# Sums over states taken first by the scheduler, four products in a row, in a decoder layer with a state-space scan

## The chip, the core and the metric

The kernel runs on one core of a Trainium2 chip. A core has five engines that work side by side, each on its own queue: PE (TensorE, matmuls, with its weight loads shown apart as PEld), DVE (VectorE), ACT (ScalarE), POOL (GpSimd) and SP (SyncE, here the issuer of most transfers). The metric is the device time of one execution in microseconds; the number given for a kernel is the median of its runs.

## The reference

One decoder layer on 8 sequences of 512 positions with 512 channels, all in float32. It has three parts, each with a residual and a layer norm:

```python
x = _layernorm(x + mamba(x))                   # state-space layer
x = _layernorm(x + cross_attention(x, ctx))    # 16 heads of 32
x = _layernorm(x + mixture_of_experts(x))      # 32 experts, 4 for each token, and a shared one
```

The part that the change touches is the state-space layer. With 1024 inner channels d and 16 states n, over the positions t:

```python
xz = layernorm(x) @ in_proj_w;  x_main, z = split(xz)
x_main = silu(conv(x_main))
dt, B_ssm, C_ssm = split(x_main @ x_proj_w);  dt = softplus(dt @ dt_proj_w + dt_proj_b)
dA  = exp(A * dt)                              # for each channel and state
dBx = dt * B_ssm * x_main
h_t = dA_t * h_(t-1) + dBx_t                   # for each channel and state
y_t = sum over n of h_t[d, n] * C_t[n]
y = (y + x_main * D) * silu(z)
out = y @ out_proj_w
```

## The kernel before

**How the work is tiled.** The scan goes through 16 chunks: 8 sequences, each in two chunks of T = 256 positions. A chunk has 32 steps (q, g, jj). q (4 values) picks 256 of the 1024 channels, g (4 values) picks one state out of each of four groups, and jj (2 values) picks half of the channels of q. One tile h of a step has 128 partitions, 32 channels times 4 state groups, and 4 blocks of 256 positions beside one another, each with one column in front for the carried state.

**A step** is a chain on three engines. `decays` (ACT, line 482, four instructions) makes exp(A dt) in one of two buffers `das`. `carry` (ACT, line 490) takes a new h buffer, one of six, and puts the carried state in its first columns. `steps_in` (DVE, line 496) writes dt B x into h. `scan` (DVE, line 503) runs the recurrence over the whole tile. `keep` (ACT, line 508) saves the last column. `collect` (DVE, line 512) multiplies h by C in place.

**The sums over states.** `collect` is called with jj = 0 and then with jj = 1. The first call only remembers h; the second hands back a function, `products`, that is called one step later. It sums over the states with PE: `fold` is a 128 x 32 matrix of ones and zeros that adds the four state groups of each channel. A group has four products of line 523 ("quarters"). Quarters 0 and 1 read the h of jj = 0, quarters 2 and 3 that of jj = 1, and quarter j writes the 32 partitions from 32 j on of the PSUM tile `py`. Over the four g the products add up in `py`, and before the first of them one product with the identity (line 521) starts it from x D. There is one `py` buffer; `gated` (DVE, line 537) multiplies z by it when all four g are in, and then the next q may start. Each float32 matmul is recorded as two instructions, so 256 groups of four products are 2048 records. An h buffer is free for `carry` and `steps_in` of a later step when its quarters have read it.

**What runs beside the scan.** In the main loop each step also issues parts of other work, in three thirds (`run(0)`, `run(1)`, `run(2)`): the next chunk's norm, transposes, input projection (line 345) and convolution (379), the products for dt (`prepare`, line 439, for the next q), the output projection of the chunk before (554), and the cross attention, gate and shared expert of the sequence before. Of the attention, `maximum` makes scores on PE (816) and takes their maxima on DVE (818), `subtract` sends the maxima back into a row of the queries by a transfer, `weigh` makes the scores again (833) and their exponentials on ACT (837), and `gather` multiplies by the values (849); the values tile has columns of ones, so that the sums of softmax come out of the same product and reach their place by transfers (869, 871). Dense products of attention and the shared expert are line 752. The parts are paced by hand: each has a weight, and a step issues as many as its share of the two chunks allows.

**What sets the order.** The program is written in one stream, and a scheduler fixes the order of every engine's queue when the kernel is built. It steps through the program in a model of the chip, and among the instructions of an engine that are ready in it takes the one with the best priority; without more said, that is the earliest in the program. On the chip each queue then runs in the fixed order, and an instruction that waits for another engine holds those behind it. Here `products()` stands after `run(1)` of the step that follows its `collect`, so what the parts of `run(2)` and of the next `run(0)` and `run(1)` put on PE is earlier in the program than the products.

Of the kernel before, what the change touches and what calls it, by code (L numbers as in the profile page):

```python
# [30 lines left out]
NQ = 4  # L31
# [55 lines left out]
def layers(ctx, tc, a, x1d, filld, based, xbuf):  # L87
# [23 lines left out]
    nc = tc.nc  # L111
# [374 lines left out]
    def carry(t, q, g, jj):  # L486

        last = state[:, q, g, jj].unsqueeze(2)
        h = mp.tile([P, NB, T + 1], F32, tag="h", name="h", bufs=6)
        nc.scalar.copy(h[:, :, 0:1], last if t else nothing)  # L490
        return h
# [18 lines left out]
    def collect(f, q, g, jj, h):  # L510

        nc.vector.tensor_tensor(h[:, :, 0:T], h[:, :, 1:], f["bc", g][1], ALU.mult)  # L512
        if jj == 0:
            f["half"] = h
            return
        hs, xs = (f.pop("half"), h), f["xs"][q]

        def products():
            if g == 0:
                f["py"] = psy.tile([P, 2, T], F32, tag="py", name="py")  # L520
                nc.tensor.matmul(f["py"], ident, xs, start=True, stop=False)
            for j in range(NQ):
                nc.tensor.matmul(  # L523
                    f["py"][j * QP : (j + 1) * QP, :, :],
                    fold,
                    hs[j // 2][:, 2 * (j % 2) : 2 * (j % 2) + 2, 0:T],
                    start=False,
                    stop=g == NG - 1,
                )

        return products

# [170 lines left out]
    def sources(b):  # L703

        st, todo = {}, []

        def begin():
            load("Wv")
            st["cT"] = cT = quad("s2", "cT")
            nc.sync.dma_start(cT, rows(a["ctx"][b]))  # L710
            st["mk"] = mk = p1.tile([P, S], U8, tag="mk", name="mk")
            nc.sync.dma_start(mk, a["mask"][b : b + 1, :].to_broadcast([P, S]))
            kept[b] = [dp.tile([S, D], F32, tag="vd", name="vd"), dp.tile([D, S], F32, tag="kd", name="kd")]

        def values(pc):
            if pc == 0:
                load("Wk")
            w, cT = loaded["Wv"], st["cT"]
            ps = dense(lambda dc: cT[:, dc, pc * P : (pc + 1) * P], lambda dc: w[:, dc, :])

            def put():
                v = p3.tile([P, D], F32, tag="row", name="v")
                nc.scalar.copy(v, ps)
                nc.sync.dma_start(kept[b][0][pc * P : (pc + 1) * P, :], v)

            return put

        def keys(oc):
            if oc == 0 and b:
                load("Wq")  # L730
            w, cT = loaded["Wk"], st["cT"]
            ps = dense(lambda dc: w[:, dc, oc * P : (oc + 1) * P], lambda dc: cT[:, dc, :])

            def put():

                k = p3.tile([P, D], F32, tag="row", name="k")
                nc.vector.scalar_tensor_tensor(k, ps, bk[:, oc : oc + 1], st["mk"], ALU.add, ALU.mult)
                nc.sync.dma_start(kept[b][1][oc * P : (oc + 1) * P, :], k)

            return put  # L740

        todo.append((0, begin, False))
        for j in range(SC):
            todo.append((3.4, lambda j=j: values(j), False))
        for j in range(DC):
            todo.append((3.4, lambda j=j: keys(j), False))
        return todo
# [298 lines left out]
    def do(fn, *args, first=False):  # L1046

        if first:
            dry(False)
        rest = fn(*args)  # L1050
        settle()
        if rest:
            left.append(rest if isinstance(rest, tuple) else (0, rest))
# [6 lines left out]
    def work(k):  # L1060

        front = 6.9 if k in (2, 3) else 3.4 if 4 <= k < 8 or k in (12, 14, 17, 20, 23) else 1.0 if k in (11, 25) else 0.0
        return 1.2 + front
# [24 lines left out]
    ahead, products = carry(0, 0, 0, 0), None  # L1088
# [3 lines left out]
    for i, (b, t) in enumerate(chunks):  # L1092
        nf = {}
        after = chunks[i + 1] if i + 1 < len(chunks) else None
        if t == 0:
            side, spent = units(b - 1) if b else sources(0), 0.0

            own = [work(k) for k in range(len(steps))] * 2
            whole = sum(own) + sum(x[0] for x in side)
        for k, (q, g, jj) in enumerate(steps):  # L1100
            if i and k == 1:
                bcast(f, NG - 1)
            if after and 28 <= k < 31:
                bcast(nf, k - 28)
            qf, nq = (f, q + 1) if q + 1 < CC // 2 else (nf, 0)
            h = ahead

            parts = []

            def part(fn, *args, first=False):  # L1110
                parts.append((do, fn, *args, first))

            if k in (2, 3) and old:
                part(back, k - 2, *old)
            if 4 <= k < 8:
                part(gate_x, k - 4, f)
            if k == 8:
                parts.append((finish_silu, f["zs"]))
            if k % 8 == 0 and q + 1 < CC // 2:
                part(prepare, q + 1, f)  # L1120
            if k == 25 and after:
                part(prepare, 0, nf)
            if after:
                if k == 8:
                    part(norm_x, nf)
                if k == 11:
                    for j in range(DC // 2):
                        part(flip_x, j, nf)
                if k in (12, 14, 17, 20):
                    part(convolve, after[1], (12, 14, 17, 20).index(k), nf, first=(k == 12))  # L1130
                if k == 22:
                    parts.append((finish_silu, *nf["xs"].values()))
                if k == 23:
                    part(x_proj, nf)
            if side and (k >= 4 or t and k < 2):
                at = t * len(steps) + k + 1
                while side and spent + sum(own[:at]) <= whole * at / len(own):
                    w, fn, alone = side.pop(0)
                    spent += w
                    part(fn, first=alone)  # L1140
            thirds = [[], [], []]
            for m, x in enumerate(parts):
                thirds[round((m + 0.5) * 3 / len(parts) - 0.5) if x[0] is do else 1].append(x)

            def run(m):
                clock[0] += 1
                settle()
                for x in thirds[m]:
                    if x[0] is do:
                        do(*x[1:-1], first=x[-1])  # L1150
                    else:
                        x[0](*x[1:])

            steps_in(f, q, g, jj, h)
            more = qf is f or after
            if k % 8 == 6 and more:
                repeat(qf, nq, 0, 1)
            if k % 8 == 1:
                if k > 1:
                    gated(q - 1, f)  # L1160
                elif old:
                    gated(CC // 2 - 1, old[2])
            if i == 0 and k == 0:
                load("Wo")
            if i == 0 and k == 2:
                biases()
            if k == 0 and old:
                twice_x(*old)
            if k == 5 and after:
                load_x(*after, nf)  # L1170
            run(0)
            scan(das[n % 2], h)
            n += 1

            if k + 1 < len(steps) or after:
                then = steps[(k + 1) % len(steps)]
                ahead = carry(t if k + 1 < len(steps) else after[1], *then)
                decays(f if k + 1 < len(steps) else nf, *then, das[n % 2])
                if k % 8 == 5 and more:
                    repeat(qf, nq, 0, 0)  # L1180
                    repeat(qf, nq, 1, 0)
                if k % 8 == 6 and more:
                    repeat(qf, nq, 1, 1)
            if held:
                keep(*held)
            held = t, q, g, jj, h
            run(1)

            if products:
                products()  # L1190
            products = collect(f, q, g, jj, h)
            run(2)
            while i < 2 and cleared < E * (i * len(steps) + k - 6) // (2 * len(steps) - 7):
                clear(cleared)
                cleared += 1
        while t and side:
            _, fn, alone = side.pop(0)
            do(fn, first=alone)
        old = (b, t, f)
        f = nf  # L1200
# [356 lines left out]
```

## Time and profile before

| | |
|---|---|
| median of 3 runs | 5468.24 us (5460.69 to 5471.74) |
| profiled execution | 5457.57 us, span 5455.9 us |
| mean granted TensorE clock | 0.925 |
| PE busy in the span | 4714.7 us (86%), 17064 instructions |
| DVE busy | 4212.0 us (77%), 5257 instructions |
| ACT busy | 2561.9 us (47%), 5617 instructions |
| stage of the scans | from the start to 3565 us |
| experts and last norm | from about 3850 us to the end |

The span is the time from the first to the last instruction; the execution has 1.7 us around it. The shares are means over stages with different limits: in the scan stage DVE is the busier engine, in the experts' stage PE. Of the six line numbers of a scan step, 482, 490 and 508 are ACT's, 496, 503 and 512 DVE's; 521 and 523 are PE's. A wait in the profile is idle time of an engine, put down to the instruction that ended it.

### The profile page before, as it was taken

To read this page: it belongs to the slowest core of one execution; us is meant where nothing else is said; L and a number is where in the kernel's file an instruction comes from. 1 tells how busy PE (TensorE), PEld (TensorE's weight loads), DVE (VectorE), ACT (ScalarE), POOL (GpSimd) and SP (SyncE) were. 2 spreads that over 40 slices of the span, in tenths; PEclk is the share of its full clock that TensorE was granted. 3 is DMA by queue.
4 is the path that set the end of the run, shared out by engine and by line. 5 is a ranking of instruction groups with operands and counts; after the bars stand their busy time and mean duration, and the time that the engine had idled before them with its cause. 6 is when DMAs were issued, how large, how long until landed. Compare 5 with 4: busy or idle time off the path is not lost. (4 is left out here: it accounts for less than half of the span.)

```text
span 5455.9 us, 53341 instructions
## 1 busy us (share of the span) xinstructions
PE 4714.7 (86%) x17064; PEld 2524.5 (46%) x17064; DVE 4212.0 (77%) x5257; ACT 2561.9 (47%) x5617; POOL 487.8 (9%) x428
## 2 busy tenths in 40 slices
PE   6768888888888888988888888788999999999994
PEld 3324334334433423433343342333677777777773
DVE  7999888888988989898898898943465556665554
ACT  5566465555655556555565655512222222222223
POOL 1000001001000100100100010010111111111111
PEclk8879989899998998998898998898999999999997
DMA  8875336345444634634543463441344444444444
GB/s 239 266 215 145 96 91 203 76 121 162 120 106 111 197 77 108 191 92 107 171 123 98 107 195 77 106 141 48 119 124 125 121 118 120 127 127 120 128 114 143
DMA packets 500889, 719.53 MB, mean 132 GB/s; under 512 B 130577, under 2 KB 215089, under 8 KB 498560
## 3 DMA queue, kind: packets, MB, share of 16 engines
q1 hardware_dynamic: 464592, 627.68, 40.1%
q0 software_dynamic: 33280, 76.90, 7.3%
q10 hardware_dynamic: 2736, 11.54, 0.5%
q8 instruction: 136, 2.23, 0.2%
q14 instruction: 145, 1.19, 0.1%
HBM read 399.63 MB, written 165.31 MB: 104 GB/s over the span
## 5 line engine op out<-in xcount | busy, mean ns | idle before, releaser
L482 ACT ACTIVATE l_da<-rep,l_aneg 128x256 f32<-128x256 f32 x2048 | 897.5, 500 | 886.0 <-DVE h L503 791.7
L503 DVE TENSOR_TENSOR_SCAN h<-l_da,h 128x1028 f32<-128x1028 f32 x512 | 1165.4, 2290 | 6.8 <-ACT l_da L482 3.9
L496 DVE TENSOR_TENSOR h<-rep,bc 128x1024 f32<-128x1024 f32 x512 | 613.0, 1216 | 132.5 <-PE py L523 78.2
L512 DVE TENSOR_TENSOR h<-h,bc 128x1024 f32<-128x1024 f32 x512 | 618.1, 1215 | 1.4
L816 PE MATMUL ps_s<-l_ka,l_qa 64*128 64x512 f32 x1024 | 349.8, 762 | 206.7 <-DVE mx L818 202.0
L523 PE MATMUL py<-h,l_fold 128*32 128x512 f32 x2048 | 400.6, 665 | 95.4 <-DVE h L512 90.7
L1307 PE MATMUL ps_h<-xT,w 128*128 128x320 f32 x1536 | 436.2, 434 | 0.0
L1387 POOL DMA_INDIRECT based<-y,xe x160 | 255.4, 1597 | 1311.5 <-ACT y L1410 578.8
L818 DVE TENSOR_REDUCE mx<-ps_s 128x2 f32<-128x1024 f32 x256 | 309.6, 1215 | 64.1 <-PE ps_s L816 62.1
L1328 DVE TENSOR_TENSOR hT<-ps_h,p 128x320 f32<-128x320 f32 x128 | 63.0, 492 | 378.9 <-PE ps_h L1307 378.9
L1307 PEld LDWEIGHTS ps_h<-xT,w 128*128 128x128 f32 x1536 | 292.7, 191 | 118.5 <-issue 0.8
L816 PEld LDWEIGHTS ps_s<-l_ka,l_qa 64*128 64x128 f32 x1024 | 144.0, 316 | 418.7 <-DVE mx L818 325.2
L837 ACT ACTIVATE eT<-ps_t 128x1024 f32<-128x1024 f32 x256 | 259.7, 1014 | 149.0 <-PE ps_t L833 148.0
L833 PE MATMUL ps_t<-l_qa,l_ka 64*128 64x512 f32 x1024 | 305.8, 675 | 26.5 <-ACT eT L837 13.6
L849 PE MATMUL po<-eT,l_va 128*64 128x512 f32 x1024 | 296.0, 658 | 32.3 <-ACT eT L837 28.7
L1307 PE MATMUL ps_h<-t,s 128*128 128x320 f32 x1024 | 286.1, 432 | 0.0
L345 PE MATMUL ps_z<-xnT,wm 128*128 128x256 f32 x1024 | 241.1, 392 | 22.0 <-DVE o L563 15.8
L554 PE MATMUL po<-wm,zs 128*128 128x512 f32 x512 | 240.2, 620 | 21.8 <-DVE z L950 13.5
L345 PE MATMUL ps_x<-xnT,wm 128*128 128x256 f32 x1024 | 251.9, 399 | 4.3 <-ACT xnT L334 2.5
L345 PEld LDWEIGHTS ps_x<-xnT,wm 128*128 128x128 f32 x1024 | 198.7, 198 | 84.7 <-issue 36.3
L345 PEld LDWEIGHTS ps_z<-xnT,wm 128*128 128x128 f32 x1024 | 195.9, 195 | 87.4 <-DVE o L563 29.2
L752 PE MATMUL ps_p<-x2T,wa 128*128 128x512 f32 x512 | 235.6, 613 | 0.7 <-DVE hT L935 0.7
(227 smaller groups left out, 7116.1 us busy)
## 6 DMA issues: line engine op xcount, KB each, us to landing
w<-in_w SPq DMA_DIRECT2D x93, 1024.0 KB
wm<-in_in_proj_w SPq DMA_DIRECT2D x128, 512.0 KB
rep<-dt SPq DMA_DIRECT2D x256, 256.0 KB
rep<-dtx SPq DMA_DIRECT2D x256, 256.0 KB
xbuf<-zero SPq DMA_DIRECT2D x32, 1362.5 KB
xe<-xbuf SPq DMA_DIRECT2D x32, 1362.5 KB
wm<-in_out_proj_w SPq DMA_DIRECT2D x64, 512.0 KB
wa<-in_sw SPq DMA_DIRECT2D x24, 1024.0 KB
```

The lines of the kernel that those rows point to most:

```text
L345: nc.tensor.matmul(ps[:, i, :], w[:, dc, i * P : (i + 1) * P], f["xnT"][:, dc, :], start=(dc == 0), stop=(dc == DC - 1),)
L482: nc.scalar.activation(da[:, n, 1:], dt[:, j, i, :], AF.Exp, scale=aneg[:, 2 * q + i, 2 * jj + j, g : g + 1])
L496: nc.vector.tensor_tensor(h[:, :, 1:], dtx.rearrange("p j i t -> p (j i) t"), f["bc", g][0], ALU.mult)
L503: nc.vector.tensor_tensor_scan(flat, da.rearrange("p n t -> p (n t)"), flat, 0.0, ALU.mult, ALU.add)
L512: nc.vector.tensor_tensor(h[:, :, 0:T], h[:, :, 1:], f["bc", g][1], ALU.mult)
L523: nc.tensor.matmul(f["py"][j * QP : (j + 1) * QP, :, :], fold, hs[j // 2][:, 2 * (j % 2) : 2 * (j % 2) + 2, 0:T], start=False, stop=g == N ...
L816: nc.tensor.matmul(ps[:, j, :], own, ka[r, :], start=True, stop=True)
L818: return lambda: nc.vector.tensor_reduce(mx[:, :, lt].unsqueeze(2), ps, AX.X, ALU.max) and None
L833: nc.tensor.matmul(ps[:, j, :], ka[r, kc * P : (kc + 1) * P], qa[r, :], start=True, stop=True)
L837: nc.scalar.activation(eT, ps, AF.Exp)
L849: nc.tensor.matmul(po[j * 2 * HD : (j + 1) * 2 * HD, :], va[:, kc, i, j * HD : (j + 2) * HD], eT[:, j, :], start=(kc == 0), stop=(kc == SC ...
L1307: nc.tensor.matmul(ps, w[:, n, r * P : (r + 1) * P], x[:, n, :], start=not more and n == 0, stop=n == 1, skip_group_check=more,)
```

## The change

```diff
             if g == 0:
                 f["py"] = psy.tile([P, 2, T], F32, tag="py", name="py")
                 nc.tensor.matmul(f["py"], ident, xs, start=True, stop=False)
-            for j in range(NQ):
-                nc.tensor.matmul(
+
+            def quarter(j):
+                return nc.tensor.matmul(
                     f["py"][j * QP : (j + 1) * QP, :, :],
                     fold,
                     hs[j // 2][:, 2 * (j % 2) : 2 * (j % 2) + 2, 0:T],
                     start=False,
                     stop=g == NG - 1,
                 )
+
+            with tc.issue_after(quarter(NQ - 1).ins):
+                for j in range(NQ - 1):
+                    quarter(j)
...
             if products:
-                products()
+                with tc.high_priority():
+                    products()
             products = collect(f, q, g, jj, h)
```

The four products of a group are issued in the order 3, 0, 1, 2. `issue_after` puts the three behind the first in PE's queue: an order of issue, not a wait for its end. Quarter 3 reads the h of jj = 1, so no product of a group is issued before both h are there. `high_priority` gives all that `products()` issues, the product with the identity among it, a priority ahead of everything else: the scheduler takes it as soon as it is ready in its model. The products of the very last step, after the loop, are called without it. What is computed, the tiles and their number of buffers stay as they are.

## The prediction

> **What bounds the kernel now.** I read the busy time by stage first. Its columns are the stretch, its length, the busy microseconds of PE (matmuls), PEld (weight loads), DVE, ACT and POOL with counts, then the granted clock and the DMA figures.
>
> ```profile
> 0.00:400.00 400.00, 270.22 (x820) 121.76 (x822) 359.47 (x358) 236.98 (x569) 31.96 (x54) 0.79 0.84 243
> 400.00:3565.00 3165.00, 2674.55 (x9280) 1169.97 (x9277) 2835.43 (x3016) 1815.66 (x4000) 168.60 (x179) 0.92 0.46 125
> 3565.00:3850.00 285.00, 237.26 (x714) 102.00 (x713) 94.14 (x165) 56.40 (x70) 31.83 (x35) 0.89 0.33 110
> ```
>
> The scans run until 3565 us; what follows (the last sequence's attention, the experts, the last norm) holds no product of line 523, so the change acts on the first two rows. From 400 on, where attention runs between the scan steps, DVE is busy 2835.43 of 3165 us (90%) and PE 2674.55 (85%). DVE is the longer queue, and it stands idle for 3165 - 2835.43 = 329.6 us. In the first 400 us there is hardly any attention beside the scans; once they have started, DVE has no gap worth a change.
>
> Second, the costly groups, which give the pace of a scan step:
>
> ```profile
> L503 DVE TENSOR_TENSOR_SCAN h<-l_da,h 128x1028 f32<-128x1028 f32 x512 | 1165.4, 2290 | 6.8 <-ACT l_da L482 3.9
> L496 DVE TENSOR_TENSOR h<-rep,bc 128x1024 f32<-128x1024 f32 x512 | 613.0, 1216 | 132.5 <-PE py L523 78.2
> L523 PE MATMUL py<-h,l_fold 128*32 128x512 f32 x2048 | 400.6, 665 | 95.4 <-DVE h L512 90.7
> ```
>
> The scan itself hardly waits. The multiplication that opens a step (496) waits 132.5 us, and 78.2 of it is for the products: it writes one of six h buffers, which is free only when the products have read it. The 2048 product records are 256 groups of four products, two records to a product.
>
> Third, who waits for whom. The first three lines are DVE's from 45 to 3565 us, the fourth is PE's over the same time, the fifth PE's from 45 to 400 us (total us, times, longest):
>
> ```profile
> DVE h L496 <- PE py L523: 78.2, 48, 4.5
> DVE h L496 <- DMA rep<-dtx: 47.0, 11, 12.1
> DVE mx L818 <- PE ps_s L816: 24.7, 38, 1.3
> ...
> PE ps_s L816 <- DVE mx L818: 195.3, 96, 5.3
> ...
> PE py L523 <- DVE h L512: 80.0, 28, 8.2
> ```
>
> PE waits for DVE's maxima 195.3 us, and DVE waits for PE's products: each stands still while work that the other needs is queued behind. ACT's copy of the carried state (490) waits another 136.1 us for the same products, 100 times, but ACT is busy 58% of the stage and the scan waits only 3.9 us for it.
>
> Fourth, PE's order of time in the middle of a sequence:
>
> ```profile
> 1459.65 1.06 PE L523 MATMUL py<-h,l_fold 128*32 128x512 f32 x8
> 1460.65 1.13 PE L833 MATMUL ps_t<-l_qa,l_ka 64*128 64x512 f32 x4
> ...
> 1467.74 1.25 PE L816 MATMUL ps_s<-l_ka,l_qa 64*128 64x512 f32 x4 [2.67 <-DVE mx L818]
> 1468.92 1.04 PE L523 MATMUL py<-h,l_fold 128*32 128x512 f32 x2
> 1469.89 1.13 PE L833 MATMUL ps_t<-l_qa,l_ka 64*128 64x512 f32 x4
> ...
> 1475.01 1.06 PE L523 MATMUL py<-h,l_fold 128*32 128x512 f32 x6
> 1476.00 1.25 PE L816 MATMUL ps_s<-l_ka,l_qa 64*128 64x512 f32 x4
> ```
>
> Two things are to be seen. Four products in a row (x8) hold PE from 1459.65 to 1460.65, 1.00 us. One alone (x2, at 1468.92) holds it 0.97 us, and its three sisters (x6, at 1475.01) 0.99: they run side by side, and a group that is torn apart costs 0.97 + 0.99 - 1.00 = 0.96 us more. And the group torn here had its second h ready at 1437.56 (end of its multiplication, line 512, in DVE's order of time): it ran 31 to 38 us late, behind attention work, 2.67 us of it spent waiting for a maximum. At 1476.10 DVE starts the 496 that had waited for it. Read off for all 256 groups, the products end 21 us after their second h on the mean, and 30 to 40 us late through the middle of every sequence; 63 groups are torn.
>
> **The change, part by part.** No instruction is added or removed and no DMA moved by hand. The order on the queues changes.
>
> (a) Products first. The wait of 496 (78.2) and that of 537, the gating that reads py (7.2 in all, 6 times), sum to 85.4 us of DVE idleness. With the products next on PE as soon as h is ready, six buffers are ample: a group needs two, and a lag of a few us replaces one of 30. I take the whole 85.4 as removed. Bounds: 0, if DVE only moves on to the next thing that PE brings late, and 85.4.
>
> (b) What is late next. PE's other work now lies behind each group. What DVE needs next of PE is above all the scores for a maximum (816 to 818). Today 38 of the 224 maxima in this stage find PE late, 17%. 223 groups start after 400 us; if 17% of them push a score by their 1.00 us in front of a waiting maximum, that is 223 x 0.17 x 1.00 = 38 us back. Bounds: nothing, if DVE is busy elsewhere each time, and 223 us, if each group does it. I take 38, since the share comes from the same wait.
>
> (c) Four side by side. 63 x 0.96 = 60 us less PE time. I cost it at nothing: the cover is DVE's 2835 us against PE's 2675. If PE set the end it would be worth up to 60.
>
> (d) The wait added. Quarters 0 and 1 read the first h and could start early; now all four wait for the second. PE stands at the group until line 512 is done, and attention's matmuls, the projections and the dt products (439) queue behind; DVE's maxima, ACT's exponentials and the next pair's dt wait for those. The trace has such waits in plenty from 45 to 400 us: 80.0 us in 28, 2.9 each, and DVE lost nothing by them, since nothing behind was due. After 400 us they are 90.7 - 80.0 = 10.7 us in 39 - 28 = 11, 1.0 each. At 1.0 for 223 groups PE is held 223 us, against 3165 - 2675 + 60 = 550 us of idle time: hidden. At 2.9 it is 647, which is 97 more than there is. I take the nearer row, after 400 us, where attention runs: nothing on the path. The range keeps the 97.
>
> A cost of holding PE is its clock. The rows above grant 0.79 in the first 400 us with PE idle a third of the time, 0.92 afterwards with 15% idle. Were the clock of the long stretch to fall to 0.79, its 2675 - 60 us would become 2615 x 0.92 / 0.79 = 3045, still under 3165: no cost by itself, but it uses up most of PE's slack. The Trainium skill ("TensorE: Matmul & The Clock Gate", Part 1) puts it otherwise: the clock drops by half only after an idle window of about 3.4 us. By that rule holds of 1.0 or 2.9 us would leave the clock alone and this item would be zero. The mean clock in these rows cannot tell the two apart.
>
> The sum: -85 + 38 + 0 + 0 = -47 us. The profiled execution has a span of 5455.9 and 5457.6 with what lies around it, so 5411 for such a run. The median of the runs, 5468.2, stands 10.7 above it; I put the forecast against the median: 5468 - 47 = **5421 us**.
>
> **The rivals.**
>
> *The wait only moves.* PE still takes everything else in its old order, and the next pair's dt (439, then ACT, DVE and a transfer) is queued among it. DVE arrives sooner and waits for the transfers of dt and dtx (47.0 us now), for line 455 (38.0) or for scores. For it: PE's backlog of 30 us is attention work, which does not shrink. Against it: much of that backlog is PE waiting 195.3 us for maxima that a freer DVE would give sooner. If all 85 come back: 5468, give or take 15.
>
> *PE is held at its head* (the slower side). By (d), if the mean hold of a group passes (3165 - 2615) / 223 = 2.5 us, PE becomes the bound of the stage. At 2.9 the end moves by 97: 5565; halfway between hold and slack, about 5510. For it: the 28 early waits are that long, and a group now has to follow DVE closely. Against it: those early waits stood where PE had nothing else to do, and the order is chosen so that other work fills the time before h is ready.
>
> *Attention slips past the scans.* Scans that no longer brake for PE can outrun attention's share. What is left at 3565 us runs in a stage where PE is busy 237 of 285 us (83%) and DVE a third: each us of slipped PE work costs 1 / 0.83 = 1.2 there. The stretch from 400 on holds seven of the eight sequences, 2615 / 7 = 374 us of PE for each; a fifth of one slipping, 75 us, costs 90 and gives 5421 + 90 = 5511. It outweighs the gain from 47 / 1.2 = 39 us on.
>
> *It does nothing*: the new order turns out as the old, since buffers rather than preference set it: 5468. The 30 us of lateness speak against that.
>
> **How the numbers follow.** Chances: forecast 0.50, wait only moves 0.16, PE held 0.17, attention slips 0.14, nothing 0.03. A measurement of this kernel can tell about 0.2%, 11 us, from no change. The forecast is faster throughout; of the moved wait I give 0.05 to faster, 0.05 to no difference and 0.06 to slower; the held PE and the slip are slower; doing nothing counts as no difference. So faster 0.55, no difference 0.08, slower 0.37. The forecast's own range is 5468 - 85 - 38 = 5345 (all of (a), none of (b), and 38 of the 60 in (c)) to 5457. For 8 in 10 the range must reach the slower cases too: up to 5540, which takes in the slip and most of the held PE short of its end of 5565.
>
> **What would show it.** Right: the wait of 496 for py falls from 78.2 to under 15 us, and ACT 490's from 136.1 with it; every group stands as x8; the lag of a group behind its second h falls from 21 us to a few; DVE's idle time from 400 us on falls from 330 to about 280; the wait of 818 for scores rises from 25 towards 60. Wrong: PE's wait at 523 for line 512 rises from 91 us past 500 (held PE), or the last scan ends sooner while the expert stage starts no sooner (slip), or the waits on dt, dtx and 455, 85 us now, double (moved).

## The result and the profile after

| | before | after |
|---|---|---|
| median | 5467.5 us (4 runs) | 5833.7 us (4 runs, 5826.8 to 5845.7) |
| ratio | | 1.0673, 95% interval 1.0652 to 1.0695 |
| profiled span | 5455.9 us | 5844.0 us |
| first to last scan | 3494 us | 3876 us |
| what follows the last scan | 1899 us | 1906 us |

The forecast was 5421 us, with 5345 to 5540 as its range. The kernel became 366 us slower by the medians. The two profiled executions differ by 388 us, and 382 of it lies between the first and the last scan. The busy time by stage of the changed kernel, columns as in the prediction:

```profile
0.00:400.00 400.00, 240.63 (x818) 121.14 (x818) 359.29 (x357) 236.38 (x568) 31.24 (x54) 0.77 0.85 243
400.00:3945.00 3545.00, 2770.04 (x9235) 1207.09 (x9231) 2839.89 (x2970) 1904.38 (x4047) 151.61 (x179) 0.87 0.41 111
3945.00:4240.00 295.00, 249.51 (x758) 106.95 (x758) 103.68 (x210) 62.95 (x77) 31.84 (x35) 0.90 0.33 110
```

DVE has the same work as before (2839.89 against 2835.43 us) in 3545 us in place of 3165: 705 us of idle time in place of 330. PE is busy 2770 us where it was 2675, at a clock of 0.87 where it had 0.92, though no group but one of the 256 is torn any more (63 before). Two engines are idle more, and none is nearer to being the bound.

The costly groups (the line of the products is now 524, later lines move by 5 or 6):

```profile
L503 DVE TENSOR_TENSOR_SCAN h<-l_da,h 128x1028 f32<-128x1028 f32 x512 | 1164.5, 2291 | 5.6 <-ACT l_da L482 1.8
L496 DVE TENSOR_TENSOR h<-rep,bc 128x1024 f32<-128x1024 f32 x512 | 612.9, 1217 | 307.3 <-DMA rep<-dtx 260.3
L524 PE MATMUL py<-h,l_fold 128*32 128x512 f32 x2048 | 342.4, 756 | 366.5 <-DVE h L512 350.5
```

DVE's instructions last as long as they did (the products' mean is 756 ns where it was 665); the idle time before 496 went from 132.5 to 307.3 us, and it ends with another event. Who waits for whom, DVE's lines and then PE's:

```profile
DVE h L496 <- DMA rep<-dtx: 260.3, 49, 10.0
DVE dtx L459 <- ACT dtx L455: 85.4, 20, 7.4
DVE hT L940 <- PE ps_p L757: 77.0, 12, 11.2
DVE zs L542 <- PE py L524: 63.1, 33, 5.1
DVE h L496 <- PE py L524: 47.0, 13, 5.5
DVE mx L823 <- PE ps_s L821: 45.7, 37, 4.3
...
PE py L524 <- DVE h L512: 350.5, 156, 14.5
PE ps_s L821 <- DVE mx L823: 104.1, 68, 4.8
```

The wait of 496 for the products fell from 78.2 to 47.0 us, but that of the gating (542) for them rose from 7.2 to 63.1. Above both stands what had been 47.0: dtx, spread over the partitions by a transfer, arrives late; and 459, a link of the chain that makes dtx, waits 85.4 us in place of 38.0. A dense product of the shared expert (into `hT`, 940) makes DVE wait 77.0 us where it was 5.6.

One such place, at the end of a q. PE's order of time in the changed kernel:

```profile
1625.90 1.25 PE L821 MATMUL ps_s<-l_ka,l_qa 64*128 64x512 f32 x4
1627.08 0.69 PE L439 MATMUL ps_dt<-xd,l_w_dt 32*128 32x256 f32 x2
1629.90 1.94 PE L524 MATMUL py<-h,l_fold 128*32 128x512 f32 x8 [2.12 <-DVE h L512]
1631.77 1.22 PE L439 MATMUL ps_dt<-xd,l_w_dt 32*128 32x256 f32 x2
```

and DVE's over the same stretch and what follows:

```profile
1628.62 1.22 DVE L512 TENSOR_TENSOR h<-h,bc 128x1024 f32<-128x1024 f32 x1
...
1637.13 0.69 DVE L459 SCALAR_TENSOR_TENSOR dtx<-dtx,u 128x512 f32<-128x512 f32 x1 [4.51 <-ACT dtx L455]
...
1640.53 0.69 DVE L462 TENSOR_TENSOR dtx<-dt,xs 128x512 f32<-128x512 f32 x1
...
1646.63 1.23 DVE L823 TENSOR_REDUCE mx<-ps_s 128x2 f32<-128x1024 f32 x1 [4.27 <-PE ps_s L821]
...
1655.98 1.23 DVE L496 TENSOR_TENSOR h<-rep,bc 128x1024 f32<-128x1024 f32 x1 [4.29 <-DMA rep<-dtx]
...
1658.26 2.29 DVE L503 TENSOR_TENSOR_SCAN h<-l_da,h 128x1028 f32<-128x1028 f32 x1
```

The second product for dt (439) stands behind the group, and the group waits 2.12 us for the last h of this q. Only then, with no scan left to run, can the chain go on: ACT, DVE's 459 to 462, the transfers, 496 at 1655.98. The last scan began at 1626.29 and the next begins at 1658.26. Before the change the products for dt of the same q went through PE while four more groups were still to come. These are PE's groups from there to the end of the q:

```profile
1489.74 1.12 PE L439 MATMUL ps_dt<-xd,l_w_dt 32*128 32x256 f32 x4
...
1502.55 1.06 PE L523 MATMUL py<-h,l_fold 128*32 128x512 f32 x8
...
1518.15 1.07 PE L523 MATMUL py<-h,l_fold 128*32 128x512 f32 x8
...
1536.31 1.06 PE L523 MATMUL py<-h,l_fold 128*32 128x512 f32 x8
...
1557.06 1.06 PE L523 MATMUL py<-h,l_fold 128*32 128x512 f32 x8
```

Two readings of the traces carry the rest. The **distance** of dt is how many groups of four stand in PE's queue between the products for dt of a q and the first group that needs them. The **idle time where a q begins** is DVE's between the start of the last scan of one q and of the first of the next, over the last 59 of the 64 beginnings (in these two kernels the earlier ones have none). Their relation, mean us at each rounded distance, number of places in brackets:

| distance | before | after |
|---|---|---|
| 0 | none | 21.5 (13) |
| 1 | none | 14.4 (7) |
| 2 | none | 7.8 (13) |
| 3 | none | 0.1 (6) |
| 4 | 3.4 (21) | 1.6 (16) |
| 5 | 1.8 (35) | 0 (1) |
| over 5 | 0 (3) | 0 (3) |
| sum of all | 134 us | 507 us |

Row 1 after the change holds six places like the one shown, with one of the two products for dt in front of the last group and one behind it; elsewhere in this text such a place counts as 0.

The sum grew by 373 us. DVE's waits during the scans grew by 367 (319 to 686). The loss stands where a q begins: outside of these stretches DVE waits 187 us before and after the change. Inside them, after the change, 207 us of waiting end with dtx's transfer and 75 with 455. The shared expert's product (77), the gating (63) and the scores (43) come late in the same stretches, in which DVE has no scan to run.

### The profile page after: what moved, and what is told of

Read it like the earlier page. It is cut to its first block, busy times and chain, and to the rows that moved or that the text cites. A ratio compares the mean times of both kernels' runs of the same rounds, so it can differ in the third digit from the quotient of the medians.

```text
span 5844.0 us, 53267 instructions
## 1 busy us (share of the span) xinstructions
PE 4793.5 (82%) x17064; PEld 2567.4 (44%) x17064; DVE 4226.9 (72%) x5257; ACT 2656.4 (45%) x5670; POOL 470.0 (8%) x428
## 5 line engine op out<-in xcount | busy, mean ns | idle before, releaser
L496 DVE TENSOR_TENSOR h<-rep,bc 128x1024 f32<-128x1024 f32 x512 | 612.9, 1217 | 307.3 <-DMA rep<-dtx 260.3
L524 PE MATMUL py<-h,l_fold 128*32 128x512 f32 x2048 | 342.4, 756 | 366.5 <-DVE h L512 350.5
L838 PE MATMUL ps_t<-l_qa,l_ka 64*128 64x512 f32 x1024 | 345.8, 682 | 21.0 <-ACT eT L842 21.0
L854 PE MATMUL po<-eT,l_va 128*64 128x512 f32 x1024 | 314.7, 681 | 22.8 <-ACT raw L866 21.4
L524 PEld LDWEIGHTS py<-h,l_fold 128*32 128x32 f32 x2048 | 47.9, 120 | 565.6 <-DVE h L512 465.8
L345 PE MATMUL ps_x<-xnT,wm 128*128 128x256 f32 x1024 | 274.8, 423 | 11.7 <-DVE xr L911 8.0
L345 PEld LDWEIGHTS ps_x<-xnT,wm 128*128 128x128 f32 x1024 | 211.8, 212 | 116.3 <-issue 53.3
```

The costliest lines, as they stand in the source:

```text
L345: nc.tensor.matmul(ps[:, i, :], w[:, dc, i * P : (i + 1) * P], f["xnT"][:, dc, :], start=(dc == 0), stop=(dc == DC - 1),)
L496: nc.vector.tensor_tensor(h[:, :, 1:], dtx.rearrange("p j i t -> p (j i) t"), f["bc", g][0], ALU.mult)
L524: return nc.tensor.matmul(f["py"][j * QP : (j + 1) * QP, :, :], fold, hs[j // 2][:, 2 * (j % 2) : 2 * (j % 2) + 2, 0:T], start=False, stop ...
L838: nc.tensor.matmul(ps[:, j, :], ka[r, kc * P : (kc + 1) * P], qa[r, :], start=True, stop=True)
L854: nc.tensor.matmul(po[j * 2 * HD : (j + 1) * 2 * HD, :], va[:, kc, i, j * HD : (j + 2) * HD], eT[:, j, :], start=(kc == 0), stop=(kc == SC ...
```

## The experiments

Ratios are to the kernel before on the same chip.

**One half of the change alone.** priority_alone drops the order inside a group:

```diff
-            with tc.issue_after(quarter(NQ - 1).ins):
-                for j in range(NQ - 1):
-                    quarter(j)
+            for j in range(NQ):
+                quarter(j)
```

> The changed kernel without the order inside a group: the four quarters go 0 to 3, each as soon as its own h is ready, still with priority over everything. Theory A (the products for dt, line 439, fall behind the last groups of the q before, so that the chain 439, 449 to 455, 459 to 462 and the transfer of dt and dtx is served when no scan is left to run): in PE's queue they stand 2.2 groups ahead of the first group that needs them, 20 of 64 at no distance, as in the changed kernel (2.5, 20); so about as slow, 5780 to 5900, and DVE's wait at 496 for dtx stays above 200 us (260 in the changed kernel, 47 before). Theory B (PE held by a whole group that waits for its second h is what costs): quarters 0 and 1 no longer wait, half of PE's 350 us at 524 for 512 goes, and so does half of the loss: about 5650.

Measured 5818.1 us, 1.0645 (1.0627 to 1.0663). The priority alone is nearly the whole loss, as theory A has it. PE's wait at the products for 512 fell by a quarter, to 263 us, and the time hardly moved. The idle time where a q begins is 522 us, near the 507 of the changed kernel, with 190 groups torn. The granted clock is that of the kernel before (0.924 against 0.925), so the loss does not need the lower clock of the changed kernel.

grouping_alone keeps that order and calls `products()` without `tc.high_priority()`.

> The changed kernel without the priority: quarters 0, 1 and 2 behind quarter 3, all in their old place in the program. Theory A: the products for dt stand 4.6 groups ahead as before the change, so the time stays at 5430 to 5500, or falls a little by the 63 groups that are no longer torn. Theory B: all four quarters wait for the second h, so a good part of the loss of 366 us is back: 5600 or more.

Measured 5501.5, 1.0073 (1.0056 to 1.0090): 37 us lost, just above what A allows and far from B. PE's idle time at the products rises from 91 to 151 us during the scans, and 57 groups are still torn: behind the fourth quarter the other three have no preference over other work.

**Less priority.** priority_60 has `tc.high_priority(60)`.

> The changed kernel, with the products moved ahead by 60 instructions of the program (not quite a step) in place of to the front of all. In PE's queue the products for dt then stand 3.9 groups ahead on the mean, 1 of 64 at no distance. Theory A: most of the loss goes, 5400 to 5520, and 496's wait for dtx falls under 100 us. Theory B: a group still waits for its second h as a whole, PE's wait at 524 for 512 stays near 350 us and the time over 5700.

Measured 5682.4, 1.0396 (1.0379 to 1.0414): too slow for A, too fast for B. The trace shows why it tells little: 125 groups are torn, and PE is busy 3099 us during the scans where it was 2897. whole_60 below repeats it without that.

**dt moved forward in the changed kernel.** dt_first_too puts the matmul of line 439 under `with tc.high_priority():`.

> The changed kernel with line 439 given the same priority as the products. The products for dt stand 3.1 groups ahead, 7 of 64 at no distance (2.5 and 20 in the changed kernel). Theory A: a good half of the loss goes: 5500 to 5680, and 496's wait for dtx falls from 260 us to 80 to 150. Theory B: PE's holds at the groups are as they were, so 5780 or more. Theory C (SP's queue, where the transfers of dt and dtx stand behind transfers that wait for maxima and softmax's sums, is what makes them late): 439 earlier helps only in part, and 496's wait for dtx stays near 200 us.

Measured 5711.2, 1.0449 (1.0431 to 1.0466): 122 us back, a third, less than A expected. 496's wait for dtx fell to 139 us, as A and not C had it, but 459 waits 98.7 us for ACT, since only the first link was moved.

chain_first moves the whole chain, through a wrapper that also covers the work handed on:

```diff
+    def early(fn):
+        def run(*args):
+            with tc.high_priority(600):
+                rest = fn(*args)
...
-                part(prepare, q + 1, f)
+                part(early(prepare), q + 1, f)
```

(and so for norm_x, flip_x, convolve, x_proj and the next chunk's prepare.)

> The changed kernel with the whole of what makes dt and x for the scans (norm, transposes, input projection for x, convolution, lines 402 and 439 with the work of ACT and DVE behind them) moved ahead by 600 instructions of the program. In PE's queue the products for dt stand 3.9 groups ahead, 7 of 64 at no distance. Theory A: more comes back than the 122 us that line 439 alone gave: 5480 to 5640, with 496's wait for dtx under 100 us. Theory D: what is brought forward puts back other work, and the time stays near 5700.

Measured 5693.6, 1.0424 (1.0398 to 1.0451). Only 140 us came back, and theory D was nearer: the idle time where a q begins fell from 507 to 280 us, but DVE now waits 100 us for the output projection and 87 for the gate's logits. One place in each of six sequences still had no distance, at 29 us each.

chain_alone has the same wrapper in the kernel before.

> The kernel before with that chain moved ahead by 600 instructions, and the products and their order as they were. The products for dt stand 5.6 groups ahead. Theory A: dt was early enough in most places before (4.6), so little is left to gain: 5400 to 5480. Theory D: any such preference disturbs the pace: 5550 or more.

Measured 5597.0, 1.0242 (1.0217 to 1.0268), against A's expectation. Bringing the chain forward costs 134 us. Dt is earlier on the mean, but one place in each of six sequences falls to distance 1 and stands idle 15.6 us, and the idle time where a q begins rises from 134 to 163 us. The larger part of the loss is elsewhere: 496's wait for the products rises to 140 us and the maxima's for scores to 92. So such a preference can cost by more than dt's place.

**dt moved back in the kernel before.** dt_late:

```diff
-            if k % 8 == 0 and q + 1 < CC // 2:
+            if k % 8 == 4 and q + 1 < CC // 2:
...
-            if k == 25 and after:
+            if k == 28 and after:
```

(with the transfers of line 430 one step later.)

> The kernel before, without priority and without grouping; only the call that makes dt for the next q comes four steps later in the program (at the fifth step of a q in place of its first), and the transfers that spread dt and dtx one step later. In PE's queue the products for dt then stand 2.3 groups ahead, 7 of 64 at no distance and 7 at one (before: 4.6, one at none; changed kernel: 2.5, 20). Theory A (dt late in PE's queue costs the time): 5620 to 5800, with 496's wait for dtx over 120 us. Theory D (it is the priority's disorder among all other work, and dt's place is only a sign of it): 5450 to 5550.

Measured 5722.1, 1.0479 (1.0452 to 1.0505): theory A. No product of line 523 was moved, and the idle time where a q begins is 486 us: 19.8 us at distance 0, 8.9 at 1, 6.9 at 2, 7.1 at 3 and 0.6 at 4. The 26 places at distance 3 cost far more here than the six after the change (0.1), so the distance is a guide and no exact price. The later place of the transfers is not what costs: SP issues the first transfer of dtx 1.6 us after dtx is ready on the mean, and in the kernel before it is 3.1 us.

**SP's queue.** spread_on_pool issues line 430 from `nc.gpsimd`.

> The changed kernel with the transfers that spread dt and dtx (line 430) issued by POOL's queue, out of SP's, where in one place of the trace dtx is ready at 1641 us and its transfer is issued at 1651, behind transfers that wait for a maximum and for softmax's sums. Theory C (SP's queue makes them late): half or more of the loss goes, 5650 or less. Theory A: the chain is late by its first matmul; up to 10 us for each of some 40 late places comes back at the most and likely a third of it, so 5700 to 5830.

Measured 5964.1, 1.0919 (1.0888 to 1.0950): neither. The order on PE changed with it (26 places at no distance), so it doesn't say what SP's queue costs. In the place shown above dtx was ready at 1641.2 us, and SP issued it at 1650.8, after transfers for softmax's sums (876) and for a maximum (830):

```profile
1647.97 0.63 SPq L876 DMA_DIRECT2D few<-raw  x1
1648.70 2.02 SPq L830 DMA_DIRECT2D l_qa<-mx  x2
1650.77 1.30 SPq L430 DMA_DIRECT2D rep<-dtx  x2
```

What taking only that away would give was not tried. But on the mean the first transfer of dtx is issued 3.1 us after dtx is ready in the kernel before and 3.3 us in the changed one, so this delay is not what the change added.

**Groups never torn, at four places.** The three quarters behind the fourth go ahead of everything, and the fourth decides the place:

```diff
-            with tc.issue_after(quarter(NQ - 1).ins):
+            with tc.issue_after(quarter(NQ - 1).ins), tc.high_priority():
```

whole_old_place calls `products()` without priority, whole_60 and whole_200 with 60 and 200, and whole_later calls it after `run(2)`.

> Groups never torn, in the old place: quarter 3 has the priority of its place in the program, and quarters 0 to 2, queued behind it, go ahead of everything. The products for dt stand 4.5 groups ahead, as before (4.6). Theory A: no loss from dt; the 60 us of PE that 63 torn groups cost are saved, and each group waits for its second h; 5440 to 5500, near the 5501 of grouping alone or better. Theory B: a whole group that waits costs, 5550 or more.

> As whole_old_place, with the products called after run(2) in place of before it, a third of a step later in the program. The products for dt stand 4.8 groups ahead. Theory A with the brake (before the change the scans are held by late products, through the six h buffers, at the pace of PE's other work): a shade later changes little, 5430 to 5500, with 496's wait for the products at 80 us or above. If lateness of the products is a loss by itself, as the prediction had it: above whole_old_place by 10 us or more.

> As whole_old_place with the group moved ahead by 60 instructions. The products for dt stand 3.8 groups ahead, as in priority_60, but no group is torn, which took PE 200 us there. Theory A: DVE's idle time where a q begins is near the 229 us of priority_60 (134 before), so 95 us of loss less what the untorn groups save: 5500 to 5580, against 5682 with torn groups. If the priority costs by something other than dt's place and the torn groups: near 5682.

> As whole_60, moved ahead by 200 instructions. The products for dt stand 2.7 groups ahead, 7 of 64 at no distance and 14 at one (changed kernel: 2.5, 20 and 1). Theory A: between whole_60 and the changed kernel, near the latter: 5720 to 5820, DVE idle at the beginnings of q 350 to 500 us.

| kernel | us | ratio | distance, mean | idle where a q begins | scans |
|---|---|---|---|---|---|
| whole_later | 5433.9 | 0.9942 (0.9927 to 0.9956) | 4.8 | 116 us | 3484 us |
| before (63 groups torn) | 5464 | 1 | 4.6 | 134 | 3494 |
| whole_old_place | 5510.8 | 1.0084 (1.0069 to 1.0098) | 4.5 | 189 | 3551 |
| whole_60 | 5579.0 | 1.0202 (1.0184 to 1.0220) | 3.8 | 225 | 3616 |
| whole_200 | 5694.9 | 1.0418 (1.0400 to 1.0435) | 2.7 | 424 | 3725 |
| after | 5833.7 | 1.0673 (1.0652 to 1.0695) | 2.5 | 507 | 3876 |

The order of the times in this table is that of the idle times. whole_later and whole_60 fell within A's range (496's wait for the products, expected at 80 us or above in whole_later, is 67); whole_old_place was 11 us slower than its range and whole_200 25 us faster. whole_old_place against whole_later is the finest step: the beginnings of a sequence stand at distance 3 in the one, with 9.5 us of idle time each, and at 4 in the other. Earlier products were slower at every step. Torn groups cost beside this: priority_60 and whole_60 have nearly the same idle time where a q begins (229 and 225 us) and differ by 103 us.

**The changed kernel with dt's place restored.** behind_dt:

```diff
+        newest[:] = [made.ins]
...
-                with tc.high_priority():
+                with tc.high_priority(), tc.issue_after(newest[0]):
                     products()
```

> The changed kernel, priority and grouping as they are, with one edge more: each group is queued on PE behind the newest product for dt (line 439) that the program has called, which is the next q's from the first group of a q on. The products for dt then stand 4.8 groups ahead, none of 63 under 4 (changed kernel: 2.5, 20 at none). Theory A (dt's place): most of the 366 us comes back: 5430 to 5560, DVE's idle time where a q begins falls from 507 us to 110 to 200, and the groups run late again by 15 us or more. Theory D (the wait moves to whatever else PE brings late, as in chain_first): 5600 to 5720, with DVE idle elsewhere.

Measured 5532.3, 1.0135 (1.0118 to 1.0151). `newest` holds the last matmul of line 439. One edge in PE's queue gives back four fifths of the loss (301 us between the medians), as A expected and D did not. The idle time where a q begins is 73 us, less than expected; the shared expert's product and the gating no longer end waits in these stretches. The edge works by holding the groups back, so this run alone does not part dt's place from later products; dt_late, in which no product is moved in the program, does. Here the groups run 15.3 us behind their second h (5.6 in the changed kernel, 23.8 before, means from 400 us on). What is left has moved to the products again:

```profile
DVE h L499 <- PE py L527: 121.8, 33, 9.6
DVE h L499 <- DMA rep<-dtx: 72.6, 21, 10.6
```

**Is later better by itself?** later_third_torn calls the products of the kernel before after `run(2)`; whole_step_later calls those of whole_later one step later again.

> The kernel before with the products called after run(2) in place of before it, quarters 0 to 3 each as soon as its h is ready, no priority: only the later place. If the later place is what gains: 5435 to 5455. If whole_later gains by groups that are no longer torn, against whose cost in whole_old_place the later place only helps: 5455 to 5480, as before.

> whole_later with the products called one whole step later again, and the gating (542) that reads their sum one step later too. The products for dt stand 5.0 groups ahead (4.8 in whole_later). If lateness goes on gaining: 5400 to 5430. If the six h buffers, which brake the scans, set a bound: 5440 to 5520, with 496's wait for the products rising from 67 us past 100.

Measured 5483.4, 1.0038 (1.0026 to 1.0050), and 5432.6, 0.9941 (0.9928 to 0.9954). The later place alone loses a little, with 81 groups torn; together with whole groups it gains 30 us, and a further step gains nothing more: 496's wait for the products is 68 us in whole_step_later, 67 in whole_later. Neither expectation of either run was met exactly. The idle time where a q begins is 57 us in whole_step_later and 116 in whole_later, at the same time, and 73 in behind_dt, which is 100 us slower: where it is this small, other waits set the time. Why whole groups lose in the old place and gain in the later one is settled only as far as the distances above go.

## Why the prediction was wrong, by its own steps

**(a) Products first, 85.4 us removed: wrong.** The two waits sum to 47.0 + 63.1 = 110.1 us. And the premise failed: the lateness of the products, 21 us on the mean, was read as a loss. Every kernel in which they end more than a microsecond earlier was slower (4.6 to 22.4 us behind their second h from 400 us on, against 23.8 before), and the two that gained have them at 23 us. Still later ones, at 24.5 to 25.1 (grouping_alone, later_third_torn, priority_60), gained nothing. The lateness looks like a brake: with six h buffers scans can run three groups ahead and no further, so PE's other work, dt's products among it, kept pace with them in program order. That fits the runs, but none changed the number of buffers, so it is argued and not shown.

**(b) What is late next: the right line, too small a circle.** The scores' wait rose by 45.7 - 24.7 = 21 us where 38 was allowed. But the next thing late was not the scores.

**(c) Four side by side at nothing: right in kind.** All groups but one are whole. PE still has more busy time than before, since its clock fell from 0.92 to 0.87 in the long stretch: 2615 x 0.92 / 0.87 = 2765 us, and 2770 was measured.

**(d) "I take the nearer row ... nothing on the path": the step that failed.** It named the dt products (439) among what queues behind a held group and "the next pair's dt" among what waits, and then priced only PE's total: 223 us of holds against 550 of slack. From 400 us on the holds came out at 249.6 us in 132, 1.9 each, near that price and well inside the slack; they would have been hidden if it were only a matter of sums. What failed is the wait for dt, put at nothing. It is set by what stands behind the last group of a q: a chain of some 25 us from 439 to 496 that DVE can't go on without. In the changed kernel distance 0 costs 20 us, 2 some 8 and 4 some 2, 507 us in all where it was 134. And it is the place that the priority gives to the products, not the wait for a whole group, that made dt late: priority_alone has the loss without the grouping, grouping_alone a tenth of it.

The rival *the wait only moves* had the mechanism, dt and line 455, and the wrong size: it took what had been removed, 85 us, as the most that could come back. The loss goes by the length of the chain instead, at 59 beginnings of a q with up to 29 us of idle time each. The test it gave, "the waits on dt, dtx and 455, 85 us now, double", was passed fourfold: 260.3 + 85.4 = 345.7 us. *PE held at its head* expected PE to become the bound; it is busy 78% of the long stretch. *Attention slips past the scans* is excluded: 1906 us after the last scan against 1899.

## What to carry to other kernels

A late consumer that holds buffers may be what keeps a fast chain in step with everything that it will need; before moving it forward, look for what the chain needs next from the same in-order queue, and count how many places ahead that stands. Price a wait at the head of a queue by the longest chain that starts behind it, not by the engine's idle share. Where several short products must stay together, the preference can go to the ones that follow, with the first left in its place; no group was torn then, though it was worth time only in the later place (0.6% gained, against 0.8% lost in the old one).

## What was not expected of the hardware

A held PE is often slow afterwards. The group at 1629.90 above, after 2.12 us of waiting, lasted 1.94 us where a group lasts 1.06, and the two records of 439 behind it 1.22 where they had lasted 0.69. The clock figure, third from the right, shows why:

```profile
1626.18:1629.59 3.41, 1.60 (x6) 0.56 (x6) 3.27 (x3) 0.20 (x1) 0.00 (x0) 1.00 0.32 95
1629.59:1636.42 6.83, 6.52 (x18) 1.50 (x18) 2.08 (x3) 3.70 (x9) 0.00 (x0) 0.50 0.14 49
```

From 400 us on, 74 of 224 groups of the changed kernel have a product of over 0.9 us (0.6 is usual), 35 before; of 58 groups right behind a gap of 1.5 to 2.5 us 30 do, and of 38 behind a gap of 0.5 to 1.5 us none. The Trainium skill ("TensorE: Matmul & The Clock Gate", Part 1) has the clock at half after an idle window of about 3.4 us. These traces agree with the 3.4 us, since the granted clock changes only on a fixed grid of 3.41 us steps, but the step before need not be idle. From 400 us to the last scan of the changed kernel, the clock fell to half after all 96 steps at the full clock in which PE was busy under 40% of the time, after 29 of 45 with 40 to 50%, and after 7 of 634 with more; in the kernel before after 57 of 57, 24 of 36 and 6 of 680. Before 1629.59 PE was busy 1.60 of 3.41 us, 47%. So in these kernels it is the sum of the gaps in a step that counts, not one long gap alone.
